# Building neighbour lists for a four-layer graph attention network: five kept row buffers, another place for one step and for the checks

## The chip, the cores and the metric

The kernel runs on one core of a Trainium2 chip. A core has five instruction engines, each with its own order of work: TensorE (PE in the profile, its weight loads PEld), VectorE (DVE), ScalarE (ACT), GpSimd (POOL) and SyncE (SP, which here only issues transfers). Data lies in SBUF and PSUM on the core and in HBM off it; transfers (DMA) are issued by an engine and run beside it. The metric is device time in microseconds (us), one number per execution.

## The reference

Four graph attention layers, each as "x = x + GAT(relu(layernorm(x)))", over one graph of 3327 nodes with 512 features. The adjacency matrix is int32, symmetric, with self loops; an edge is there with a chance of about 0.0048, so a node has some 17 neighbours, itself among them. The layers differ in their heads (8, 4, 1, 8), in the form of the weights, and in an ELU after the middle two.

```python
adj = (bernoulli(0.0024, (3327, 3327)) | its transpose | eye).astype(int32)

def gat(h, adj, W, a_src, a_dst):                 # one layer, one head shown
    Wh = h @ W
    e = leaky_relu((Wh @ a_src)[:, None] + (Wh @ a_dst)[None, :], 0.2)
    e = where(adj > 0, e, -inf)
    return softmax(e, over the neighbours) @ Wh   # then elu in layers 1 and 2

for i in range(4):
    h = maximum((x - mean) / sqrt(var + 1e-5), 0)
    x = x + gat(h, adj, *weights[i])
```

## The kernel before

The nodes are padded to 3328 and handled as 26 tiles of 128 rows, one row to an SBUF partition. Rather than work with the dense matrix, the kernel first turns it into lists of neighbours (`tile_gat_stack`, from L521), then runs the four layers by gathering the rows of neighbours from tables in HBM (`tile_gat_lists`). If the lists could not be right for the matrix at hand (a node with over 40 neighbours, too many nodes with many neighbours, or an entry that isn't 0 or 1), a dense version, `tile_gat_dense`, runs instead. A flag `bad`, computed with the lists, chooses between them.

**The list loop, L677 to L719.** For each tile t:

- SyncE loads the 128 adjacency rows `a` (1664 KB, three buffers, L682), and GpSimd multiplies them by `keys`, which fall from left to right: `key` (L683, three buffers) is 0 where there is no edge and names the column where there is one. VectorE adds BOOST on the diagonal, so that a node itself comes first (L687). ScalarE sums the rows of `a` into `total`, the number of neighbours (L689).
- VectorE cuts each row into 16 segments and takes the eight largest keys of each (L692, into `cand`). Between these 16 instructions stand the *pieces* of the tile before, made by `rest` (L653): nine in turn take the 40 largest out of its `cand` (`max` at L659, `match_replace` at L661), then `counted` (L632) lets ScalarE write the list `L[:, t, :]` and VectorE count the entries found into `held`, and `sorted_in` (L637) marks the bin of that count in `o`, has TensorE form, in `pn`, how many rows with that count stand ahead of each row, and in `count`, how many rows each bin holds so far (L639 to L643); ScalarE copies `count` to `sofar` for the next tile (L646). `placed` (L651) reads `pn` for VectorE; it stands at segment 8, for the tile before the one whose pieces run.
- In the same loop the features of layer 0 are made. The row of `x` is loaded into the middle of a wide row buffer `vx` by a DMA that ScalarE issues (L709 to L711). `centred_by_scalar` (L478 to L493) finds mean and variance on ScalarE: `nm` (L485), `xn` (L487), `squares` (L490), `ve` (L492). `features` (L666 to L673) then works on the tile before: TensorE transposes `xn` (L451), ScalarE copies the result with a relu (`hT`, L458), TensorE projects (`pv`, L469), GpSimd makes `rstd` out of `ve` (L432), ScalarE writes the projected row into the same `vx` (L669, L671), and SyncE stores it into the table `tabx` in HBM (L673). `vx` comes out of a rotating pool with four buffers.

A block `tc.manual_schedule` keeps the orders of GpSimd and VectorE as written in the loop. ScalarE, TensorE and SyncE are put in order by a scheduler when the program is built. So GpSimd has key of tile t+1, rstd of tile t, key of tile t+2, and so on, in a fixed order.

**After the loop, L717.** With nothing left to be interleaved with, the last steps run on their own: `last` (which is `placed` of tile 24), the eleven pieces of tile 25, then `placed` of tile 25.

**The ranks, L720 to L783.** Here the order of all engines but SyncE is as written. VectorE adds BOOST to the first column of `L` (L722), sums the bins (scan, L723) and gives each node its rank, which is stored into `tabx` (L724 to L729); `hi` and `lo` split the rank into tile and row. Then come the checks: `held` against `total` (L741, L742), the first neighbour against the node's own number (L744, L745), the bins against their limits (L747, L748), each summed into a column of `wrong`, and from these `bad` (L753). The rest, to L783, turns lists and ranks into index tables, with which the gathers of the layers run (L830).

Of the kernel before, what the change touches and what calls it, by code (L numbers as in the profile page):

```python
# [10 lines left out]
F32 = mybir.dt.float32  # L11
# [4 lines left out]
OP = mybir.AluOpType  # L16
AX = mybir.AxisListType
# [507 lines left out]
def tile_gat_stack(ctx: ExitStack, tc: tile.TileContext, x, adj, adjT, ws, avs, out):  # L525
# [35 lines left out]
    with ExitStack() as c1:  # L561
# [92 lines left out]
        def rest(t, cand):  # L654
# [8 lines left out]
            pieces.append(lambda: made.append(sorted_in(t)))  # L663
            return pieces, lambda: placed(t, made[0])

        def features(t, vx, xn, ve):  # L666
            pv = projected(nc, W, cut(nc, turned(nc, xn, ident, ps_t), work), ps_v)
            rstd = rooted(nc, ve, small, half)
            nc.scalar.activation(vx[:, :ROW].rearrange("p (s n) -> p s n", s=2), pv[:, :, :ROW // 2], AF.Copy,  # L669
                                 scale=rstd)  # L670
            nc.scalar.activation(vx[:, ROW + F:].rearrange("p (s n) -> p s n", s=2), pv[:, :, ROW // 2 - 8:ROW // 2],  # L671
                                 AF.Copy, scale=rstd)
            nc.sync.dma_start(tabx[t * P:(t + 1) * P, :], vx)  # L673

        count, pieces, last, normed, loads = None, [], None, None, []
        with tc.manual_schedule(engines={mybir.EngineType.Pool, mybir.EngineType.DVE}):
            for t in range(NT):  # L677
                a = apool.tile([P, NP], I32, name="a")
                key = kpool.tile([P, NP], I32, name="key")
                quarter = NP // 4 if t == 0 else NP  # L680
                for c in range(0, NP, quarter):
                    nc.sync.dma_start(a[:, c:c + quarter], adj[t * P:(t + 1) * P, c:c + quarter])  # L682
                    nc.gpsimd.tensor_tensor(key[:, c:c + quarter], a[:, c:c + quarter], keys[:, c:c + quarter], OP.mult)  # L683
                if t == 1:
                    W = Weights(nc, wpool, work, 0, ws, avs)
                dg = key[:, t * P:(t + 1) * P]
                nc.vector.tensor_add(dg, dg, boost)  # L687
                waste = once.tile([P, NP], mybir.dt.bfloat16, name="waste")
                nc.scalar.activation(waste, a, AF.Relu, accum_out=total[:, t:t + 1])  # L689
                cand = small.tile([P, SEGS * 8], F32, name="cand")  # L690
                for g in range(SEGS):
                    nc.vector.max(cand[:, g * 8:(g + 1) * 8], key[:, g * SEG:(g + 1) * SEG])  # L692
                    if g == SEGS // 2 and last is not None:
                        last()
                        last = None
                    elif g > 0 and pieces:
                        pieces.pop(0)()
                if t == 0:
                    constants()
                if t == 1:  # L700
                    while W.left:
                        W.fold()
                if t == 2:
                    own = late_constants()
                if t > 0:
                    last = then
                pieces, then = rest(t, cand)

                vx = work.tile([P, 2 * ROW], F32, name="vx", bufs=4)  # L709
                xt = vx[:, ROW:ROW + F]  # L710
                nc.scalar.dma_start(xt, x[t * P:(t + 1) * P, :])  # L711
                if normed is not None:
                    features(*normed)
                normed = (t, vx, *centred_by_scalar(nc, xt, small, work))
            features(*normed)
            for piece in [last, *pieces, then]:
                piece()  # L717

        with tc.manual_schedule(engines={mybir.EngineType.Pool, mybir.EngineType.PE,  # L719
                                         mybir.EngineType.DVE, mybir.EngineType.Activation}):  # L720

            nc.vector.tensor_scalar(L[:, :, 0], L[:, :, 0], BOOST, None, OP.add)  # L722
            nc.vector.tensor_tensor_scan(base[:, 1:], ones[:, :BINS], count, 0.0, OP.mult, OP.add)  # L723
            nc.vector.tensor_mul(o, o, base[:, :BINS].unsqueeze(1).to_broadcast([P, NT, BINS]))  # L724
            rank = small.tile([P, NT], F32, name="rank", bufs=1)
            nc.vector.tensor_reduce(rank, o, AX.X, OP.add)
            nc.vector.tensor_add(rank, rank, part)

            nc.sync.dma_start(tabx[:NP, :].rearrange("(t p) c -> p t c", p=P)[:, :, F // 2:F // 2 + 1],  # L729
                              rank.unsqueeze(2))  # L730
            hi = small.tile([P, NT], F32, name="hi", bufs=1)
            nc.vector.tensor_scalar(hi, rank, 1.0 / P, -(P - 1) / 2.0 / P, OP.mult, OP.add)
            nc.vector.tensor_scalar(hi, hi, ROUND, -ROUND, OP.add, OP.add)
            lo = small.tile([P, NT], F32, name="lo", bufs=1)
            nc.vector.scalar_tensor_tensor(lo, hi, -float(P), rank, OP.mult, OP.add)

            wrong = small.tile([P, 3], F32, name="wrong", bufs=1)
            m1 = small.tile([P, NT], F32, name="m1", bufs=2)  # L740
            nc.vector.tensor_tensor(m1, held, total, OP.not_equal)  # L741
            nc.vector.tensor_reduce(wrong[:, 0:1], m1, AX.X, OP.add)  # L742
            m1 = small.tile([P, NT], F32, name="m1", bufs=2)
            nc.vector.tensor_tensor(m1, own, L[:, :, 0], OP.not_equal)  # L744
            nc.vector.tensor_reduce(wrong[:, 1:2], m1, AX.X, OP.add)  # L745
            junk = small.tile([P, BINS], F32, name="junk")
            nc.vector.tensor_tensor(junk, base[:, :BINS], limit, OP.is_gt)  # L747
            nc.vector.tensor_reduce(wrong[:, 2:3], junk, AX.X, OP.add)  # L748
            pn = ps_n.tile([P, BANK], F32, name="pn", bufs=1)
            nc.tensor.matmul(pn[0:1, :3], ones[:, 0:1], wrong, start=True, stop=True)  # L750
            worst = small.tile([1, 1], F32, name="worst", bufs=1)
            nc.vector.tensor_reduce(worst, pn[0:1, :3], AX.X, OP.max)
            nc.vector.tensor_copy(bad, worst)  # L753


            for i, part_ in enumerate(slots.parts):
                t0, t1 = min(b[0] for b in part_.blocks), max(b[1] for b in part_.blocks)
                high = fixed[:, 304:512] if i == 0 else ps_k.tile([P, BANK], F32, name="high")
                high = high[:, :NT * (t1 - t0)].rearrange("p (t h) -> p t h", h=t1 - t0)
                nc.vector.tensor_tensor(high, ahead[:, t0:t1].unsqueeze(1).to_broadcast([P, NT, t1 - t0]),  # L760
                                        hi.unsqueeze(2).to_broadcast([P, NT, t1 - t0]), OP.is_equal)
                n = part_.columns
                if i == 0:
                    (_, _, k, _), = part_.blocks
                    every = once.tile([P, NT, n], F32, name="every")
                    nc.vector.tensor_tensor(every.rearrange("p t (h k) -> p t h k", k=k),
                                            L[:, :, :k].unsqueeze(2).to_broadcast([P, NT, t1 - t0, k]),
                                            high.unsqueeze(3).to_broadcast([P, NT, t1 - t0, k]), OP.mult)
                pi = ps_i.tile([P, BANK], F32, name="pi")
                for t in range(NT):  # L770
                    if i == 0:
                        rhs = every[:, t, :]
                        nc.vector.tensor_scalar(low[:, t, :], ahead, lo[:, t:t + 1], None, OP.is_equal)
                    else:
                        rhs = spare[:, t % 2, :]
                        for b0, b1, k, c in part_.blocks:
                            nc.vector.tensor_tensor(
                                rhs[:, c:c + (b1 - b0) * k].rearrange("p (t k) -> p t k", k=k),
                                L[:, t, :k].unsqueeze(1).to_broadcast([P, b1 - b0, k]),
                                high[:, t, b0 - t0:b1 - t0].unsqueeze(2).to_broadcast([P, b1 - b0, k]), OP.mult)  # L780
                    nc.tensor.matmul(pi[:, :n], low[:, t, :], rhs, start=(t == 0), stop=(t == NT - 1))
                nc.scalar.activation(part_.idx, pi[:, :n], AF.Copy)
                nc.scalar.activation(part_.twice, pi[:, :n], AF.Copy, scale=2.0)  # L783
# [655 lines left out]
```

## Time and profile before

| | us |
|---|---|
| median of three runs | 2492.9 (2492.3 to 2494.5) |
| the profiled execution | 2493.66 |
| its span, first to last instruction | 2491.9 |
| list loop and ranks, up to the first gather on GpSimd | 282.25 |
| VectorE's first work of the layers | 307.30 |
| start of the 26th, last key of GpSimd | 243.73 |
| store of the ranks | 266.19 |

The mean granted clock of TensorE was 0.945 of full speed. A profile comes from one execution, whose span is a little shorter than its device time. Lines of groups read: line of the kernel, engine, operation, output<-inputs, shape, count; then busy time, mean ns of one; then the idle time of the engine just before these instructions and what ended it. In a timeline a line has the start in us, the duration, engine, line and operation, and in brackets the idle time before it with its releaser. "ACTq" is the issue of a transfer by ScalarE. The table of windows gives the busy time of each engine in a stretch, with the number of instructions behind "x". An idle engine costs nothing unless the end hangs on it.

Over the whole span TensorE was busy for 2083.4 us (84%), VectorE for 1935.6 (78%), GpSimd for 1710.7 (69%), ScalarE for 911.6 (37%). From 310 us on, where the layers run, TensorE was busy for 1881.4 of 2181 us.

### The profile page before, as it was taken

The numbers are of one execution on the slowest core, as the hardware profiler recorded it, in microseconds if no ns is written. First come the engines' busy times: TensorE is split into PE (matmuls) and PEld (weight loads), VectorE is DVE, ScalarE is ACT, GpSimd is POOL, SyncE is SP. The second block draws the span as 40 slices with busy tenths as digits, with TensorE's granted clock in tenths as the row PEclk, the third lists the DMA queues.
The fourth block names the chain that finished last, engine by engine and source line by source line (L and its number), as shares of the span: only waits on it lengthen the run. The fifth ranks groups of instructions, "written<-read, shape, count | busy, mean of one in ns | idle before, by whom it ended". The sixth has DMA issues, their size and how long they took to land. (4 is left out here: it accounts for less than half of the span.)

```text
span 2491.9 us, 26810 instructions
## 1 busy us (share of the span) xinstructions
PE 2083.4 (84%) x6832; PEld 1163.5 (47%) x6832; DVE 1935.6 (78%) x5004; ACT 911.6 (37%) x2506; POOL 1710.7 (69%) x1700
## 2 busy tenths in 40 slices
PE   3776789999898855999999986869696699999897
PEld 1655445555444422555555543434353454455453
DVE  7887787887767735788888876978979488787776
ACT  4777123343321102433333323433333343333330
POOL 7798367777777756776777746655546377777775
PEclk9888899999999987999999998979898899999999
DMA  6797579999887777877888858867777488888885
GB/s 231 280 298 240 173 219 291 284 298 296 277 270 237 231 194 239 261 244 228 247 258 258 252 162 264 271 194 239 211 229 212 134 253 247 246 250 250 240 243 173
DMA packets 262490, 599.55 MB, mean 241 GB/s; under 512 B 103923, under 2 KB 121331, under 8 KB 257974
## 3 DMA queue, kind: packets, MB, share of 16 engines
q0 software_dynamic: 126128, 438.08, 57.7%
q1 hardware_dynamic: 132454, 152.86, 19.2%
q10 hardware_dynamic: 3744, 6.82, 0.8%
q8 instruction: 55, 0.90, 0.1%
q14 instruction: 109, 0.89, 0.1%
HBM read 547.96 MB, written 49.65 MB: 240 GB/s over the span
## 5 line engine op out<-in xcount | busy, mean ns | idle before, releaser
L917 PE MATMUL bank<-m,ident 128*128 128x512 f32 x2608 | 1204.6, 608 | 132.6 <-DVE m L912 132.0
L912 DVE TENSOR_TENSOR m<-g,pw 128x512 f32<-128x512 f32 x1304 | 810.6, 681 | 137.3 <-ACT pw L886 131.5
L830 POOL DMA_INDIRECT g<-tab,idxb x734 | 698.2, 951 | 284.7 <-issue 173.1
L917 PEld LDWEIGHTS bank<-m,ident 128*128 128x128 f32 x2608 | 483.3, 193 | 714.0 <-issue 347.5
L469 PE MATMUL pv<-w,hT 128*128 128x264 f32 x1664 | 438.5, 420 | 67.4 <-ACT hT L458 38.8
L886 ACT ACTIVATE pw<-z 128x32 f32<-128x32 f32 (+5 forms) x434 | 84.0, 194 | 987.2 <-DVE z L885 987.1
L469 PEld LDWEIGHTS pv<-w,hT 128*128 128x128 f32 x1664 | 340.3, 208 | 170.3 <-ACT hT L458 44.1
L830 POOL DMA_INDIRECT g<-tabx,twiceb x342 | 324.2, 948 | 105.1 <-issue 78.6
L830 POOL DMA_INDIRECT g<-tab,idxa x297 | 283.6, 955 | 145.1 <-issue 78.2
L1133 PE MATMUL whole<-ve,em 128*128 128x512 f32 x468 | 222.4, 623 | 41.4 <-DVE em L1119 38.5
L883 DVE TENSOR_TENSOR z<-g,pw 128x32 f32<-128x32 f32 (+5 forms) x434 | 74.9, 173 | 189.3 <-DMA g<-tab,idxa 83.0
L683 POOL TENSOR_TENSOR key<-a,keys 128x3328 int32<-128x3328 int32 (+1 forms) x29 | 189.1, 6525 | 14.5 <-DVE cand L692 11.8
L907 DVE SCALAR_TENSOR_TENSOR bank<-g,pw,bank 128x512 f32<-128x512 f32 x243 | 183.2, 754 | 6.8
L1133 PEld LDWEIGHTS whole<-ve,em 128*128 128x128 f32 x468 | 90.1, 199 | 152.3 <-issue 90.7
L692 DVE MAX8 cand<-key 128x8 f32<-128x208 int32 x416 | 143.7, 363 | 0.1
L830 POOL DMA_INDIRECT g<-tabx,twicea x99 | 94.4, 954 | 67.8 <-issue 32.7
L451 PE MATMUL pt<-ident,xn 128*128 128x128 f32 x416 | 68.6, 291 | 85.5 <-ACT hT L458 31.0
L451 PEld LDWEIGHTS pt<-ident,xn 128*128 128x128 f32 x416 | 53.6, 149 | 122.6 <-issue 48.4
L1108 ACT ACTIVATE r<-low,mc,b 128x384 f32<-128x384 f32 x78 | 52.6, 674 | 153.5 <-DVE em L1119 116.6
L432 POOL TENSOR_TENSOR rstd<-ve,half 128x1 f32<-128x1 f32 x52 | 31.8, 611 | 107.3 <-DVE ve L970 61.7
L1242 ACT ACTIVATE r<-low,spare 128x256 f32<-128x256 f32 x208 | 98.9, 476 | 5.1
L885 DVE SCALAR_TENSOR_TENSOR z<-z 128x32 f32<-128x32 f32 (+5 forms) x434 | 78.8, 182 | 15.3 <-DVE z L883 0.4
(175 smaller groups left out, 2111.5 us busy)
## 6 DMA issues: line engine op xcount, KB each, us to landing
a<-in_adj SPq DMA_DIRECT2D x25, 1664.0 KB, 9.0
tab<-v SPq DMA_DIRECT2D x78, 264.0 KB, 4.0
ve<-tab SPq DMA_DIRECT2D x78, 264.0 KB, 4.5
g<-tab SPq DMA_DIRECT2D x66, 264.0 KB, 4.7
tabx<-vx SPq DMA_DIRECT2D x26, 528.0 KB, 9.5
g<-tab,idxb POOLq DMA_INDIRECT x734, 3.9
low<-tab SPq DMA_DIRECT2D x52, 132.0 KB, 3.4
room<-tab SPq DMA_DIRECT2D x52, 132.0 KB, 3.6
```

Of the source, the lines that this page charges most:

```text
L451: nc.tensor.transpose(pt[:, k, :], xn[:, k * P:(k + 1) * P], ident)
L469: nc.tensor.matmul(pv[:, s, :HF + 8], hT[:, k, :], W.w[:, k, s, :], start=(k == 0), stop=(k == KC - 1))
L683: nc.gpsimd.tensor_tensor(key[:, c:c + quarter], a[:, c:c + quarter], keys[:, c:c + quarter], OP.mult)
L692: nc.vector.max(cand[:, g * 8:(g + 1) * 8], key[:, g * SEG:(g + 1) * SEG])
L830: nc.gpsimd.indirect_dma_start(out=out_, out_offset=None, in_=table, in_offset=bass.IndirectOffsetOnAxis(ap=which, axis=0))
L885: nc.vector.scalar_tensor_tensor(z, z, SLOPE, z, OP.mult, OP.max)
L886: nc.scalar.activation(self.wt[:, k0:k0 + n, :H], z, AF.Exp)
L907: nc.vector.scalar_tensor_tensor(acc, v, w, acc, OP.mult, OP.add)
L912: nc.vector.tensor_tensor(m[:, q, :].rearrange("p (s h d) -> p s h d", s=2, d=D), v.rearrange("p s (h d) -> p s h d", d=D), wt[:, k0 + q, ...
L917: nc.tensor.matmul(self.po, ident, m[:, q, :], start=(k0 + q == 0), stop=(k0 + q == K - 1))
L1133: nc.tensor.matmul(tl.po.rearrange("p (s m) -> p s m", s=2), e[:, q * P:(q + 1) * P], v.rearrange("p (s m) -> p s m", s=2)[:, :, :F // 2], ...
L1242: nc.scalar.activation(self.r[:, h, :], self.a[:, g, :], AF.Relu, bias=-1.0, scale=self.b[:, j, g:g + 1])
```

## The change

Line numbers here are those of the kernel before.

1. The row buffers are no longer taken from the rotating pool of four. Five tiles `vx0` to `vx4` are kept for the whole stage, and tile t uses number t modulo 5. A list `loads` that nothing used goes.
2. After the loop, `last` no longer runs first, but as the fifth of the steps, behind the first four pieces of tile 25.
3. The boost of the first column (L722) and the first two checks (L740 to L745) become a function `check`, which runs after the pieces of tile 25 and ahead of its `placed`. So they leave the second block, in which all engines' orders are as written, for the first, in which only those of GpSimd and VectorE are. The third check and `bad` stay where they were.

```diff
+        wrong = small.tile([P, 3], F32, name="wrong", bufs=1)
+
+        def check():
+            nc.vector.tensor_scalar(L[:, :, 0], L[:, :, 0], BOOST, None, OP.add)
+            m1 = small.tile([P, NT], F32, name="m1", bufs=2)
+            nc.vector.tensor_tensor(m1, held, total, OP.not_equal)
+            nc.vector.tensor_reduce(wrong[:, 0:1], m1, AX.X, OP.add)
+            m1 = small.tile([P, NT], F32, name="m1", bufs=2)
+            nc.vector.tensor_tensor(m1, own, L[:, :, 0], OP.not_equal)
+            nc.vector.tensor_reduce(wrong[:, 1:2], m1, AX.X, OP.add)
+
...
-        count, pieces, last, normed, loads = None, [], None, None, []
+        rows = [once.tile([P, 2 * ROW], F32, name=f"vx{i}") for i in range(5)]
+        count, pieces, last, normed = None, [], None, None
...
-                vx = work.tile([P, 2 * ROW], F32, name="vx", bufs=4)
+                vx = rows[t % 5]
                 xt = vx[:, ROW:ROW + F]
                 nc.scalar.dma_start(xt, x[t * P:(t + 1) * P, :])
...
             features(*normed)
-            for piece in [last, *pieces, then]:
+            pieces[4:4] = [last]
+            for piece in [*pieces, check, then]:
                 piece()
...
-            nc.vector.tensor_scalar(L[:, :, 0], L[:, :, 0], BOOST, None, OP.add)
             nc.vector.tensor_tensor_scan(base[:, 1:], ones[:, :BINS], count, 0.0, OP.mult, OP.add)
...
-            wrong = small.tile([P, 3], F32, name="wrong", bufs=1)
-            m1 = small.tile([P, NT], F32, name="m1", bufs=2)
-            nc.vector.tensor_tensor(m1, held, total, OP.not_equal)
-            nc.vector.tensor_reduce(wrong[:, 0:1], m1, AX.X, OP.add)
-            m1 = small.tile([P, NT], F32, name="m1", bufs=2)
-            nc.vector.tensor_tensor(m1, own, L[:, :, 0], OP.not_equal)
-            nc.vector.tensor_reduce(wrong[:, 1:2], m1, AX.X, OP.add)
```

## The prediction, made before the changed kernel ran

> **What bounds the kernel now.** I first cut the run into stretches with the table of busy time by window. The list building fills the first 310 us, the four layers the rest, and the change touches only the list building. In its long middle no engine is full:
>
> ```profile
> core 0: us, PE busy (x) PEld busy (x) DVE busy (x) ACT busy (x) POOL busy (x), PEclk, DMA share, GB/s
> 90.00:243.00 153.00, 111.81 (x501) 90.97 (x500) 124.98 (x615) 120.69 (x250) 136.36 (x35) 0.87 0.83 277
> ```
>
> GpSimd (POOL) is nearest to full, 136.4 of 153 us. The groups of this window (busy, mean ns, idle before) say what it does and what it lacks:
>
> ```profile
> L683 POOL TENSOR_TENSOR key<-a,keys 128x3328 int32<-128x3328 int32 x18 | 130.6, 7254 | 0.0
> L432 POOL TENSOR_TENSOR rstd<-ve,half 128x1 f32<-128x1 f32 x17 | 9.3, 548 | 16.0 <-ACT ve L492 7.0 <-DVE cand L692 5.6 <-DVE top L659 3.2
> ```
>
> All idle time stands before `rstd`, whose only moving input is ScalarE's `ve`; the view names VectorE for part of it, but `rstd` reads nothing of VectorE's, so I book all of it to `ve`. POOL's order is fixed: key of tile t+1, rstd of tile t, key of tile t+2. POOL's timeline shows the two great holes and the small steady ones:
>
> ```profile
> 62.05 7.26 POOL L683 TENSOR_TENSOR key<-a,keys 128x3328 int32<-128x3328 int32 x1 [11.77 <-DVE cand L692]
> 78.27 0.55 POOL L432 TENSOR_TENSOR rstd<-ve,half 128x1 f32<-128x1 f32 x1 [8.95 <-DVE top L659]
> 78.78 7.25 POOL L683 TENSOR_TENSOR key<-a,keys 128x3328 int32<-128x3328 int32 x1
> ...
> 225.60 0.55 POOL L432 TENSOR_TENSOR rstd<-ve,half 128x1 f32<-128x1 f32 x1 [0.82 <-ACT ve L492]
> 226.11 7.25 POOL L683 TENSOR_TENSOR key<-a,keys 128x3328 int32<-128x3328 int32 x1
> ```
>
> ScalarE's timeline says why `ve` is late in both places:
>
> ```profile
> 66.31 0.34 ACTq L711 DMA_DIRECT2D vx<-in_x  x1
> 73.92 0.62 ACT L485 ACTIVATE waste<-vx 128x512 f32<-128x512 f32 x1
> 78.00 0.19 ACT L492 ACTIVATE ve<-squares 128x1 f32<-128x1 f32 x1
> ...
> 223.25 0.21 ACT L646 ACTIVATE sofar<-count 128x41 f32<-128x41 f32 x1 [1.74 <-PE count L643]
> 224.21 0.64 ACT L490 ACTIVATE waste<-xn 128x512 f32<-128x512 f32 x1
> 225.30 0.22 ACT L492 ACTIVATE ve<-squares 128x1 f32<-128x1 f32 x1
> ```
>
> At 66.31 the row of tile 4 is first loaded: it has to reuse the buffer of tile 0, so its `ve` is there at 78.2 and POOL has stood since 69.3. At 223.25 `squares` and `ve` of the next tile stand behind `sofar`, which waits for counts that need VectorE's work on the newest key: POOL's key ends, 7.6 us of VectorE and TensorE, 2.1 us of ScalarE, then `rstd`. That is longer than one 7.77 us turn of POOL. Last, VectorE's end of the stage, from which every later step of the lists hangs:
>
> ```profile
> 261.96 0.19 DVE L722 TENSOR_SCALAR L<-L 128x26 f32<-128x26 f32 x1
> 262.66 0.20 DVE L651 SCALAR_TENSOR_TENSOR junk<-pn,o 128x41 f32<-128x41 f32 x1 [0.50 <-PE pn L640]
> 263.10 0.24 DVE L723 TENSOR_TENSOR_SCAN base<-ones,count 128x41 f32<-128x41 f32 x1 [0.24 <-PE count L643]
> ...
> 266.72 0.18 DVE L741 TENSOR_TENSOR m<-held,total 128x26 f32<-128x26 f32 x1
> 267.36 0.19 DVE L747 TENSOR_TENSOR junk<-base,limit 128x41 f32<-128x41 f32 x1
> ```
>
> **What the Trainium skill says.** "DMA: Bandwidth & Descriptors", section "Anatomy of one DMA": a wait for a semaphore is kept on the issuing sequencer, not in the DMA engine, and one transfer costs about 2.0 us plus bytes over 436 GB/s. So a row load stands in ScalarE's own order; and 262,144 bytes make 2.6 us as an estimate, where the view of the row buffers gives 2.7 as the least. Its section "Issuing engines are not separate DMA queues" says that transfers of all issuers share the same 16 engines; the trace agrees, for beside the adjacency the same load takes 8.9:
>
> ```profile
> DMA to landing us min/median/max: 2.7/8.9/11.5
> ```
>
> "SBUF — State Buffer", section "SBUF: two separate sides": a VectorE operation with two SBUF inputs and a GpSimd operation lock each other out. It shows here (the product at 42.52 took 7.36 us against 0.69, until POOL's key was done), but the moved checks run after POOL's last `rstd` at 252.94.
>
> **Part by part.** In the built program POOL's order is the same; VectorE's differs only at the end of the stage; ScalarE's and TensorE's, which a scheduler makes, change all through. After the lists all engines keep their order, and the waits that differ there, from another memory layout, are for work long done. So what the stage saves, the run saves.
>
> *Five rows, start.* 26 loads and 26 stores as before. The fifth load goes out at the start; 256 KB beside 1664 KB that take some 4 us is at most 0.6 us for a neighbour, and POOL waits 11.8 us at 50 anyway: 0. Key 6 (78.78 before) then needs: POOL free at 69.31 plus 0.52 for rstd 4; key buffer free at 69.0 (VectorE's tile 3); adjacency of tile 6, issued 57.61, at 9.0 (its median) 66.6. So 69.8, 8.9 earlier. Key 7 needs rstd 5, and tile 5 now takes the place of tile 4 (load 66.31, `ve` 78.2), and the adjacency issued at 70.85, there at 79.5 to 79.9: start 79.5, against 87.14. Key 8 needs `ve` 6: its load now is the one of 75.42, landed 79.96; behind it in ScalarE's new order nm 0.75, total 2.96, row writes 0.75, hT 0.5, xn 0.7, squares 0.75, kept and ve 0.3, makes 86.7, and POOL is free at 86.75. Key 8 at 87.3 against 96.04: 8.7 saved.
>
> *Five rows, steady.* Before, key 8 to key 25 took 243.73 - 96.04 = 147.7, 8.69 each. In the new order `ve` t is queued behind `sofar` t-2, in places with the row write of t-1 between, instead of behind `sofar` t-1: a whole turn earlier. POOL alone needs 7.25 + 0.52 = 7.77, 17 turns 132.1. What is left of waits: ScalarE's work for a tile sums to 7.0 us (total 2.96; nm, xn, squares 2.2; row 0.75; hT 0.5; six small ones 0.6), so it has only 0.8 to spare, and between `ve` 9 and `ve` 10 its order now has two totals (11, 12). Carried from `ve` 9 at 108.6: totals 11 and 12 make 6, two row writes 1.5, hT, nm, xn, squares, hT 3.2, small ones 0.5, and 0.6 until pv 9 is ready: 120.4, where POOL is free at 117.7: 2.7. At 13, 14 and 19 to 23 `ve` slips behind the next row write, which I put at 4 together. For row loads that land later (ScalarE waited for those 14.0 us in all before) I add 3.5. Waits 10.2, key 25 at 87.3 + 132.1 + 10.2 = 229.6 against 243.73: 14.1 saved.
>
> *Last counts later.* `placed` 24 stood at 258.05, and its counts ended at 257.99: nothing to win; four pieces (1.4 us) later it has cover for TensorE's new order, where counts 24 come behind seven of eight products of tile 25. 0; without that cover some 1 us.
>
> *Checks.* Five VectorE instructions and no DMA: the boost and the four of 266.72 to 267.36, 0.64. They fill the waits of 0.50 and 0.24 before `placed` and the scan, which costs 0.1 to 0.3 there, and leave 0.64 behind the scan: 0.4 saved. But the boost reads ScalarE's list of tile 25, which is now queued behind the row write of tile 25, which needs its products. If these end as before (262.2), the boost starts at 263.4, not 261.96, and `placed` behind it at 264.4: a loss of 1.1. If the stage runs ahead, none. Between -0.4 and +1.1 I take 0.
>
> Sum: 14. The profiled execution took 2493.66 us (span 2491.9, 1.8 around it), 0.8 above the median of 2492.9; 2493.7 - 14 = 2479.7 for it, **2479** for the median. Its own range, waits from 5 to 15 us: 2474 to 2484.
>
> **Rivals.** *The rate stays at 8.69,* since ScalarE (7.0 of 7.77) or the DMAs (share 0.83 at 277 GB/s; at 7.77 it would be 0.93) pace it. For it: ScalarE's waits for row loads. Against: single turns of 7.73 and 7.92 in POOL's timeline (113.93, 121.66, 129.58). Only 8.7 is saved: 2484, 2483 to 2487. *No waits at all:* key 25 at 219.4, 24.3 saved, 2469; against it the two totals in a row. *Slower:* for tiles 17 to 21 the next row load is queued up to 2.6 us behind the nm of the row before, elsewhere right behind it (0.75), so one load is under way at a time. If a load takes 8.9 from its own issue, a turn is 11.5 for five tiles and 9.65 for twelve: 3.7 x 5 + 1.9 x 12 = 41 more on 132.1, less 4 that `ve` is ahead; key 25 at 256.6, 13 later, 2506. It decides from about 8.1 us. Against it: loads issued later than the adjacency of their turn landed sooner (issued 98.01, used 104.21; 75.42, 79.96), for they end with that burst. *It doesn't do what it says:* the scheduler's order gives the start back, within 5 us of 2493.
>
> **Numbers.** Likeliest 0.58, rate stays 0.18, no waits 0.12, given back 0.05, slower 0.07. 2470 to 2487 leaves out half of "no waits" and the last two. A change of 0.2%, 5 us, is what a measurement can tell: faster 0.88, same 0.05, slower 0.07.
>
> **What would show it.** Key 6 near 70 and key 8 near 87; rstd's idle time from key 8 on near 10 us, not 17, the largest near tile 10; the five checks ahead of the scan; 2226 us from the rank store to the end as now. I am wrong if row loads keep ScalarE waiting over 3 us a tile, or if key 6 stays at 78.

## The result: 8.0 us faster, and where they came from

| | before | changed |
|---|---|---|
| median of six runs, us | 2492.87 (2489.87 to 2494.50) | 2484.85 (2482.29 to 2489.33) |
| ratio, 95% interval | | 0.9970 (0.9958 to 0.9983) |
| profiled execution, span | 2491.9 | 2483.4 |
| key 6 of GpSimd starts | 78.78 | 70.77 |
| key 8 | 96.04 | 88.61 |
| key 25, the last | 243.73 | 236.01 |
| sum of the ranks (VectorE) | 265.98 | 258.65 |
| first gather | 282.25 | 273.46 |
| first gather to the end of the span | 2209.7 | 2209.9 |

The time was inside the forecast range of 2470 to 2487, but near the rival "the rate stays", not the likeliest case: 14 us were forecast, 8 came, and the likeliest case's own range ended at 2484. The last row of the table says where to look: behind the first gather the two kernels take the same time. All of the difference is in the list building.

The hole ahead of key 6 is gone, as the prediction had it; the one of 11.77 us ahead of key 5 is not. GpSimd's timeline of the changed kernel (start, duration, then in brackets the idle time before):

```profile
63.04 7.26 POOL L695 TENSOR_TENSOR key<-a,keys 128x3328 int32<-128x3328 int32 x1 [11.77 <-DVE cand L704]
70.26 0.54 POOL L432 TENSOR_TENSOR rstd<-ve,half 128x1 f32<-128x1 f32 x1
70.77 7.26 POOL L695 TENSOR_TENSOR key<-a,keys 128x3328 int32<-128x3328 int32 x1
...
113.95 7.27 POOL L695 TENSOR_TENSOR key<-a,keys 128x3328 int32<-128x3328 int32 x1
125.86 0.55 POOL L432 TENSOR_TENSOR rstd<-ve,half 128x1 f32<-128x1 f32 x1 [4.64 <-ACT ve L492]
126.38 7.26 POOL L695 TENSOR_TENSOR key<-a,keys 128x3328 int32<-128x3328 int32 x1
```

Before, `rstd` of tile 4 stood 8.95 us idle ahead of 78.27; here it starts as soon as the key at 63.04 is done. But further down there is a hole of 4.64 us that was not there before. To compare the steady part, take the same stretch of work of both, key 8 to key 25, in the table of busy time by window, first of the kernel before (core busy times of PE, PEld, DVE, ACT, POOL with the instructions behind "x", clock, DMA share, GB/s):

```profile
96.00:244.00 148.00, 107.86 (x487) 88.00 (x488) 121.20 (x596) 116.27 (x244) 132.29 (x36) 0.87 0.84 279
```

and of the changed one:

```profile
88.00:236.00 148.00, 115.41 (x515) 95.19 (x514) 125.29 (x617) 120.05 (x251) 132.39 (x35) 0.85 0.84 292
```

The fifth busy number is GpSimd's: 132.29 and 132.39 of the same 148 us. The groups of GpSimd in this window of the changed kernel agree:

```profile
L432 POOL TENSOR_TENSOR rstd<-ve,half 128x1 f32<-128x1 f32 x18 | 10.0, 558 | 15.6 <-ACT ve L492 11.7 <-DVE cand L704 3.4 <-DVE cand L661 0.2
```

15.6 us idle before `rstd` (16.9 before the change, over the same number of tiles). So the fifth buffer took the hole ahead of key 6 away and left the steady waits as large as they were. They are in other places, though. Before, 13 of the 17 turns had a wait of 0.5 to 2.4 us; now ten have 0.2 us or less, two have 0.8, and five hold nearly all: 1.7, 4.7, 1.4, 3.4 and 2.5 us. ScalarE's timeline at the largest (start, duration, operation) shows what stands before `ve`:

```profile
113.15 0.20 ACT L492 ACTIVATE ve<-squares 128x1 f32<-128x1 f32 x1
113.26 2.96 ACT L701 ACTIVATE waste<-a 128x3328 bf16<-128x3328 int32 x1
...
117.39 0.70 ACT L680 ACTIVATE vx<-pv,rstd 128x528 f32<-128x528 f32 x1 [0.85 <-PE pv L469]
...
119.47 0.72 ACT L487 ACTIVATE xn<-vx,nm 128x512 f32<-128x512 f32 x1
120.10 2.96 ACT L701 ACTIVATE waste<-a 128x3328 bf16<-128x3328 int32 x1
...
123.61 0.70 ACT L680 ACTIVATE vx<-pv,rstd 128x528 f32<-128x528 f32 x1 [0.24 <-PE pv L469]
...
124.49 0.63 ACT L490 ACTIVATE waste<-xn 128x512 f32<-128x512 f32 x1
...
125.58 0.21 ACT L492 ACTIVATE ve<-squares 128x1 f32<-128x1 f32 x1
```

Between `ve` 9 (113.15) and `ve` 10 (125.58) there are two sums of adjacency rows (L701) and two row writes (L680). The second sum stands between `xn` of tile 10 and its `squares`, though all that `squares` needs is there at 120.1. GpSimd had finished its key at 121.2 and stood until 125.86.

The end of the stage in the changed kernel, VectorE's timeline:

```profile
253.99 0.26 DVE L637 TENSOR_SCALAR o<-fixed,held 128x41 f32<-128x41 f32 x1
254.28 0.19 DVE L669 TENSOR_SCALAR L<-L 128x26 f32<-128x26 f32 x1
...
255.59 0.24 DVE L735 TENSOR_TENSOR_SCAN base<-ones,count 128x41 f32<-128x41 f32 x1 [0.70 <-PE count L643]
255.75 0.15 DVE L675 TENSOR_REDUCE wrong<-m 128x1 f32<-128x26 f32 x1
255.82 0.19 DVE L651 SCALAR_TENSOR_TENSOR junk<-pn,o 128x41 f32<-128x41 f32 x1
```

The boost (L669) comes right behind the pieces, with no wait for ScalarE's list; the checks fill part of the wait for the counts. From the start of key 25 to the sum of the ranks it is 22.64 us (22.25 before), to the product that opens the index tables (`every`) 24.75 (24.99 before): 0.4 longer to the one place and 0.2 shorter to the other, in one execution of each.

### The profile page after: what moved, and what is told of

The parts are those of the page before. It is cut to its first block, busy times and chain, and to the rows that moved or that the text cites. A ratio compares the mean times of both kernels' runs of the same rounds, so it can differ in the third digit from the quotient of the medians.

```text
span 2483.4 us, 26799 instructions
## 1 busy us (share of the span) xinstructions
PE 2077.1 (84%) x6832; PEld 1161.7 (47%) x6832; DVE 1935.1 (78%) x5004; ACT 910.9 (37%) x2506; POOL 1709.5 (69%) x1700
## 5 line engine op out<-in xcount | busy, mean ns | idle before, releaser
L922 PE MATMUL bank<-m,ident 128*128 128x512 f32 x2608 | 1202.3, 607 | 131.9 <-DVE m L917 131.2
```

The source lines that it names most:

```text
L922: nc.tensor.matmul(self.po, ident, m[:, q, :], start=(k0 + q == 0), stop=(k0 + q == K - 1))
```

## The experiments

A theory from these lines, "order": with five buffers GpSimd's waits are set by where ScalarE's order puts `ve`, not by how fast rows, DMA or TensorE can go. Its rival, "pace": a tile takes 8.7 us on average whatever the order, since something else holds it. A second question was which part of the change is worth what.

In the tables a wait is the distance between the starts of two keys less 7.77 us (7.25 for the key, 0.52 for `rstd`), summed over the 17 turns from key 8 to key 25. "Drain" is the time from the start of key 25 to the sum of the ranks. These come from one profiled execution of each kernel. Two kernels were run twice (e6 and e13, e9 and e12): their pairs differ by up to 0.6 us in key 25, 1.7 in the waits and 1.3 in the drain, so smaller differences tell nothing. The ratios are to the kernel before in the same session, where it took 2493.5 us beside e1, e2, e5 and e6 and 2493.4 beside e10 to e13.

| kernel | median, us | ratio to before (95%) | key 6 | key 8 | key 25 | waits | drain |
|---|---|---|---|---|---|---|---|
| before | 2492.9 | | 78.8 | 96.0 | 243.7 | 15.6 | 22.3 |
| changed | 2484.9 | 0.9970 (0.9958 to 0.9983) | 70.8 | 88.6 | 236.0 | 15.3 | 22.6 |
| e1 five rows only | 2484.9 | 0.9968 (0.9956 to 0.9981) | 70.4 | 89.3 | 236.1 | 14.7 | 22.9 |
| e2 moved steps only | 2492.8 | 0.9998 (0.9990 to 1.0006) | 79.4 | 97.2 | 243.7 | 14.4 | 23.8 |
| e5 six rows | 2495.5 | 1.0009 (1.0003 to 1.0016) | 71.1 | 86.5 | 246.2 | 27.6 | 22.5 |
| e6 five rows, ve ahead | 2477.7 | 0.9938 (0.9926 to 0.9951) | 70.8 | 87.5 | 221.3 | 1.8 | 29.0 |
| e13 the same again | 2474.8 | 0.9930 (0.9917 to 0.9943) | 70.8 | 89.0 | 221.2 | 0.1 | 27.8 |
| e12 six rows, ve ahead | 2474.6 | 0.9924 (0.9911 to 0.9937) | 71.7 | 87.2 | 219.1 | -0.2 | 27.9 |
| e11 e6 with the end reordered | 2477.2 | 0.9937 (0.9924 to 0.9950) | 70.7 | 89.4 | 222.7 | 1.3 | 27.5 |
| e10 e12 with the end reordered | 2475.6 | 0.9924 (0.9911 to 0.9937) | 71.0 | 86.5 | 222.9 | 4.3 | 27.9 |

Four runs (e3, e7, e8, e9) were made in another session, in which every kernel, the one before included, took some 3010 to 3046 us. The record names another chip for it; whether the chip as such or its condition made the difference, the runs do not tell.

| kernel | median, us | ratio to before (95%) | key 6 | key 8 | key 25 | waits | drain |
|---|---|---|---|---|---|---|---|
| before, there | 3046.4 | | | | | | |
| e3 pool of five | 3033.1 | 0.9962 (0.9941 to 0.9984) | 70.6 | 87.7 | 238.4 | 18.7 | 22.8 |
| e7 e6 with counts first | 3031.8 | 0.9956 (0.9935 to 0.9976) | 70.6 | 87.4 | 221.5 | 2.1 | 29.0 |
| e8 four rows, ve ahead | 3035.8 | 0.9974 (0.9953 to 0.9995) | 79.1 | 97.1 | 236.1 | 6.9 | 25.4 |
| e9 six rows, ve ahead | 3010.0 | 0.9889 (0.9849 to 0.9928) | 71.4 | 86.9 | 219.7 | 0.7 | 29.1 |

The list building takes there what it took in the first session (key 25 of e9 and e12, the same kernel: 219.7 and 219.1), so its positions can be compared over both tables; the layers do not, and so these four times cannot.

### e1 and e2: which part is it?

e1 gives the kernel before the five rows and nothing else. e2 is the changed kernel with the pool of four put back:

```diff
-                vx = work.tile([P, 2 * ROW], F32, name="vx", bufs=4)
+                vx = rows[t % 5]          # e1, on the kernel before, with the line that makes the five rows
...
-                vx = rows[t % 5]
+                vx = work.tile([P, 2 * ROW], F32, name="vx", bufs=4)    # e2, on the changed kernel
```

> The kernel before with the five row buffers alone; the last steps and the checks stay where they were. In the built program its ScalarE and TensorE orders are those of the changed kernel. If the fifth buffer is the whole of the gain: 2485 us, 8 under before, GpSimd's 26th key near 236 (before 243.7), key 6 near 71. If half of the gain came from the moved steps: about 2489.

> The changed kernel with the row buffers back in the rotating pool of four; only the moved step and the moved checks are left. If they are worth nothing that can be measured: 2493, within 1.5 us of before, and the VectorE work from the 26th key to the ranks as long as before within 0.5 us. If they carry half of the gain: 2489. In the trace: rank sum 0.3 to 0.4 us later behind the key, the first large product of the index tables 0.2 to 0.3 us earlier.

e1 took 2484.93 us, the whole gain; e2 2492.75, no measurable one. Both as the first branch said, but for one detail: the drain of e2 was 1.5 us longer than before to the sum of the ranks and 0.9 longer to `every` (25.9 against 25.0), where a gain of 0.2 to 0.3 was expected for the latter. Its VectorE stood 1.39 us before the last `placed` for `pn`. That is hardly more than the 1.3 us by which the drain of one kernel differs between two executions, and the time does not show it. Between e1 and the changed kernel the moved steps are worth 0.8 us to `every` (25.6 against 24.75), again inside that scatter. So the moved steps are worth nothing that can be measured; the fifth buffer is the change.

### e6: put ve ahead

One rule more for the order in which ScalarE gets its instructions, no instruction added: from tile 9 on, the sum of tile t is issued behind `ve` of tile t-1.

```diff
-                nc.scalar.activation(waste, a, AF.Relu, accum_out=total[:, t:t + 1])
+                with tc.issue_after(marks[t - 1].ins) if t > 8 else ExitStack():
+                    nc.scalar.activation(waste, a, AF.Relu, accum_out=total[:, t:t + 1])
...
-                normed = (t, vx, *centred_by_scalar(nc, xt, small, work))
+                xn, ve, done = centred_by_scalar(nc, xt, small, work)    # done: the instruction of ve
+                marks.append(done)
+                normed = (t, vx, xn, ve)
```

> The changed kernel with one more rule for the order of ScalarE: from tile 9 on the sum of adjacency rows of tile t is issued behind ve of tile t-1, so that no ve has two of these sums, or a sum and a row write, between it and the ve before. No instruction is added. Theory 'order' (the 15 us that GpSimd still waits between keys 8 and 25 come from places where ScalarE's order puts ve late): turns of 7.8 us throughout, 26th key at 223 to 227 instead of 236.0, time 2473 to 2477. Theory 'pace' (DMA at 0.84 or the chain of TensorE and ScalarE can't go faster than 8.7 us a tile): the waits come back in other places, 26th key at 234 or later, time within 3 us of 2485.

Key 25 came at 221.33, a little before the interval that "order" gave, and the waits fell from 15.3 to 1.8 us. GpSimd's groups from key 8 to key 25:

```profile
L696 POOL TENSOR_TENSOR key<-a,keys 128x3328 int32<-128x3328 int32 x18 | 130.6, 7258 | 0.5 <-DMA a<-in_adj 0.5
L432 POOL TENSOR_TENSOR rstd<-ve,half 128x1 f32<-128x1 f32 x18 | 9.8, 546 | 1.9 <-ACT ve L492 1.0 <-DVE top L659 0.5 <-DVE cand L706 0.2
```

And the window from 90 us to the last key (busy times of PE, PEld, DVE, ACT, POOL; then clock, DMA share, GB/s):

```profile
90.00:221.00 131.00, 100.56 (x478) 83.53 (x477) 121.02 (x598) 110.39 (x234) 128.78 (x34) 0.89 0.90 318
```

"Pace" falls: with the same work, GpSimd runs at 7.87 us a turn, full at 128.8 of 131 us, and the DMAs bring 318 GB/s where 292 seemed to be what they gave. The 15 us were a matter of the built order. Not of ScalarE's order alone, though: the rule names ScalarE, but the scheduler made another order for TensorE with it. In the changed kernel the counts stand in the middle of the products of most tiles. In e6 the products of tiles in the middle of the stage stand unbroken ahead of the counts (all 16 records of a tile in a row, at 113.50, 120.40, 128.74 and 135.63 us), and from key 8 to key 25 ScalarE waited 1.6 us for products, not 7.7 as in the changed kernel. What each of the two orders is worth was not separated.

The time was 2477.73 us, 7.1 under the changed kernel and just over the 2473 to 2477 expected, and 2474.84 in a second run (e13). But key 25 came 14.7 earlier. Nearly half of that went in the drain, which grew from 22.6 to 29.0 us. VectorE's timeline of e6 there:

```profile
235.90 0.20 DVE L651 SCALAR_TENSOR_TENSOR junk<-pn,o 128x41 f32<-128x41 f32 x1 [2.03 <-PE pn L640]
...
243.73 0.20 DVE L651 SCALAR_TENSOR_TENSOR junk<-pn,o 128x41 f32<-128x41 f32 x1 [3.43 <-PE pn L640]
```

VectorE waits for `pn` of tiles 23 and 24, which TensorE has behind feature products. When the last key is done (228.6), three rows of features are still to be written in e6, at 231.1, 239.0 and 245.2; in the changed kernel (243.3) it is two, at 245.2 and 251.5. Their products share TensorE with the last counts.

The same kernel once more, beside the later runs:

> Five rows with ve ahead once more, beside the others on one chip: 15 to 17 us under before as in its first run, key 25 at 221 to 223.

It came 18.5 us under the kernel before, more than expected, with key 25 at 221.2.

### e5, e9 and e12: six rows

```diff
-        rows = [once.tile([P, 2 * ROW], F32, name=f"vx{i}") for i in range(5)]
+        rows = [once.tile([P, 2 * ROW], F32, name=f"vx{i}") for i in range(6)]
...
-                vx = rows[t % 5]
+                vx = rows[t % 6]
```

> The changed kernel with six kept row buffers in turn. Theory 'order': what counts is the order that ScalarE gets with it; in the built program ve is behind a sum and a row write for tiles 12, 14, 16, 18, 20, so GpSimd waits some 5 us at each, the 26th key comes near 244 and the time is near 2493, the gain lost. Theory 'buffers' (rows still come too late with five): 2485 or less.

2495.5 us, with key 25 at 246.2: a sixth buffer loses all that the fifth gained. The waits are where the order said, 4.95, 5.17, 4.02, 4.66 and 3.76 us in five turns. ScalarE's timeline at one of them:

```profile
148.32 0.72 ACT L487 ACTIVATE xn<-vx,nm 128x512 f32<-128x512 f32 x1
154.77 2.98 ACT L701 ACTIVATE waste<-a 128x3328 bf16<-128x3328 int32 x1 [5.73 <-DMA a<-in_adj]
...
158.74 0.62 ACT L490 ACTIVATE waste<-xn 128x512 f32<-128x512 f32 x1
...
159.91 0.21 ACT L492 ACTIVATE ve<-squares 128x1 f32<-128x1 f32 x1
```

`xn` is done at 149; the sum behind it waits 5.73 us for adjacency rows, and `squares` and `ve`, which need nothing of it, wait with it. With the same six rows and the rule of e6:

> The rule of ve ahead with six row buffers kept. Theory 'order': the 27.6 us of waits that six buffers alone had were all the scheduler's order of ScalarE, so with the rule they fall under 4 us, the 26th key comes at 219 to 222 instead of 246.2, and the time is 2475 to 2479, as with five. Theory 'buffers' (a sixth load under way harms by itself, through the DMAs): waits stay over 12, time over 2484.

Key 25 came at 219.7 and the waits fell from 27.6 to 0.7: the sixth buffer does no harm by itself. The time, 36 us under before, was more than the list building can give and came from the slower session, so it was run again:

> The six rows with ve ahead once more, since its first time came from a chip on which every kernel took some 3040 us and scattered by 40. The list building there ended 19 us earlier than in the kernel before on the first chip (first gather 263.0 against 282.3). If only the list building is behind its gain: 14 to 19 us under before. If the 36 us of the first time were real: over 25 under before, on a part that the change doesn't touch.

2474.55 us, 18.8 under before, the first branch. The 36 us were not the kernel's own; what gave e9 the rest on the other chip stays open. e12 is the fastest of the kernels run, level with e13 inside the intervals.

### e8 and e3: four rows with the rule, and a pool of five

```diff
+        rows = [once.tile([P, 2 * ROW], F32, name=f"vx{i}") for i in range(4)]    # e8, with e6's rule
+                vx = rows[t % 4]
...
-                vx = work.tile([P, 2 * ROW], F32, name="vx", bufs=4)
+                vx = work.tile([P, 2 * ROW], F32, name="vx", bufs=5)              # e3, on the kernel before
```

> The rule of ve ahead with only four row buffers kept. The hole ahead of key 6 stays (key 6 near 79, key 8 near 96). If the rule works by itself, by ScalarE's order alone: waits from key 8 on fall from 15 us to some 3 to 5, 26th key at 232 to 236, and with some 6 us given back in the drain as with five buffers, time 2485 to 2489. If the rule needs the fifth buffer (rows come too late with four): waits stay over 10, time 2491 to 2494.

> The kernel before with its rotating pool raised from four buffers to five, nothing else. In the built program its orders are those of the five kept rows but for five places on ScalarE. If only the number of buffers counts: 2485 as with kept rows, 26th key near 236. If it matters that the rows are kept and taken in turn: a difference of over 2 us from 2485.

e8: key 6 stays at 79.1, and the waits fall to 6.9 us, of which 5.6 stand in one turn; more than the 3 to 5 expected, but far under the 10 of the other branch. So hole and waits are two things: with four buffers the hole stays whatever the order, and the order sets most of the waits. e3: key 6 at 70.6 and key 25 at 238.4, two us behind the kept rows and with 18.7 us of waits in nearly the same places. Times in that session can't tell 2 us. That the rows are kept, rather than dealt out by a pool, is not what helps.

### e7, e10 and e11: the drain

Three attempts to get back what the drain took. e7 has TensorE do the products of tile 24 behind the counts of tile 23 (in the code `counts[-2]` at the first place below, and `counts[-1]` round the second `features` where it stood), those of tile 25 behind the counts of tile 24. e10 and e11 (on six and on five rows) go one tile further:

```diff
-                    features(*normed)
+                    with tc.issue_after(counts[-1].ins) if t == NT - 1 else ExitStack():   # e10, e11
+                        features(*normed)
...
-            features(*normed)
             pieces[4:4] = [last]
-            for piece in [*pieces, check, then]:
+            for piece in pieces:
                 piece()
+            with tc.issue_after(counts[-1].ins):
+                features(*normed)
+            check()
+            then()
```

> The kernel with ve ahead, and one more rule: TensorE gets the products of tile 24 behind the counts of tile 23, those of tile 25 behind the counts of tile 24. With ve ahead alone the stretch from the 26th key to the sum of the ranks took 29.0 us (changed kernel 22.6, before 22.3), and VectorE stood 2.0 and 3.4 us before placed 23 and 24 for counts that were queued behind feature products. If this queue is what gave half of the gain back: the stretch shrinks to 24 to 26 us, the two waits go, time 2473 to 2476. If something else holds the end of the stage (ScalarE's last rows, the stores): the stretch stays over 28 and the time within 1.5 of 2478.

> Six rows with ve ahead, and the end of the loop reordered: TensorE gets the products of tile 24 behind the counts of tile 24 and those of tile 25 behind the counts of tile 25, so that no count is queued behind products whose own inputs are late. If that queue on TensorE is what lengthened the drain: from the 26th key to the sum of the ranks 24 to 26 us instead of 29, waits before placed 23 to 25 under 1 us each but the last, time 3 to 5 us under six rows with ve ahead. If the stores of the last rows become the end: the ranks come earlier, the first gather does not, and the time is within 1 us.

> The same end of the loop with five rows and ve ahead. From the 26th key to the sum of the ranks 24 to 26 us (29.0 with ve ahead alone); time 3 to 5 us under five rows with ve ahead, so about 18 to 20 under before. If not the queue on TensorE: 29 us again and the same time.

All three missed: drains of 29.0, 27.9 and 27.5 us, where e6 and e13 had 29.0 and 27.8 and e12 27.9. The times did not gain either: e10 took 2475.6 us beside 2474.6 for e12, e11 2477.2 beside 2474.8 for e13, and e7 has no like kernel in its session. One of e11's six executions took 5494.4 us; it is not in the median, there is no trace of it, and its cause stays open. The queue on TensorE was not the whole of it. TensorE's timeline of e11:

```profile
237.47 0.52 PE L639 MATMUL pn<-o,upper 128*128 128x41 f32 x2 [2.19 <-DVE o L637]
...
241.01 5.52 PE L469 MATMUL pv<-w,hT 128*128 128x264 f32 x16 [0.69 <-ACT hT L458]
246.37 0.31 PE L639 MATMUL pn<-o,upper 128*128 128x41 f32 x2
```

`pn` of tile 24 (237.47) now waits for VectorE, as it should. But the products of tile 24 come next, 5.5 us of them, and `pn` of tile 25, ready to go at 242, comes behind at 246.4; VectorE stood 4.03 us for it. The wait went from one tile to the next. What would clear the drain, products split around the last counts or less feature work left by then, was not tried.

## Why the prediction was right, and where it was off

**The bound was read rightly.** GpSimd's chain of keys and `rstd` set the stage, and `rstd` hung on ScalarE's `ve`. e6 shows it: with `ve` in time, GpSimd is full.

**Five rows, start: right, with one wrong zero.** Forecast were key 6 at 69.8 and key 8 at 87.3; they came at 70.77 and 88.61. About 1 us of this is the step "the fifth load goes out at the start ... POOL waits 11.8 us at 50 anyway: 0". Key 1 began at 15.25 instead of 14.38, and keys 2 to 5 were each 0.96 to 0.99 late. GpSimd's timeline has both, first of the kernel before:

```profile
14.38 7.24 POOL L683 TENSOR_TENSOR key<-a,keys 128x3328 int32<-128x3328 int32 x1 [0.44 <-DMA a<-in_adj]
```

and of the changed one:

```profile
15.25 7.23 POOL L695 TENSOR_TENSOR key<-a,keys 128x3328 int32<-128x3328 int32 x1 [1.04 <-DMA a<-in_adj]
```

The 11.77 us at key 5 are no cover. They end when VectorE has folded the weights and searched tile 2, and VectorE's own start hangs on the same early keys; so the wait moved as a whole (62.05 to 63.04) and was 11.77 us in both kernels. That the fifth load is what made the early adjacency late is likely, since every kernel with five or six rows has key 1 at 15.1 to 15.4 and those with four (before, e2, e8) at 14.4 to 14.8; the 256 KB alone make 0.65 us, as an estimate from the 406 GB/s that the DMAs moved, at a full share, from 5 to 30 us in the kernel before. SyncE's first weight loads went off at other times too (7.46 us instead of 5.66 for the first), and the two were not separated.

**Five rows, steady: the step that failed.** "Waits 10.2" was 15.3. Term by term: tile 10, the largest as forecast, was put at 2.7 and measured 4.7. The row writes ahead of `ve` (tiles 13, 14, 19 to 23), put at 4 together, measured 7.5. The 3.5 for "row loads that land later" has 3.1 to match it (tiles 7, 15 and small ones), but it was not the loads. In the stretches shown above, 96 to 244 us before and 88 to 236 us after, ScalarE's wait for row loads fell from 12.4 to 9.4 us and its wait for counts from 15.0 to 9.1, while its wait for TensorE's products, ahead of the row writes, rose from 1.9 to 7.7. Tile 21 shows it best. First TensorE's timeline, then ScalarE's:

```profile
209.88 0.71 PE L469 MATMUL pv<-w,hT 128*128 128x264 f32 x2 [2.43 <-ACT hT L458]
...
211.74 6.22 PE L469 MATMUL pv<-w,hT 128*128 128x264 f32 x14
```

```profile
212.69 2.97 ACT L701 ACTIVATE waste<-a 128x3328 bf16<-128x3328 int32 x1
...
218.05 0.70 ACT L680 ACTIVATE vx<-pv,rstd 128x528 f32<-128x528 f32 x1 [2.31 <-PE pv L469]
...
219.56 0.20 ACT L492 ACTIVATE ve<-squares 128x1 f32<-128x1 f32 x1
```

and GpSimd's:

```profile
219.84 0.55 POOL L432 TENSOR_TENSOR rstd<-ve,half 128x1 f32<-128x1 f32 x1 [2.50 <-ACT ve L492]
```

The counts stand between the two parts of the products, the row write waits 2.31 us for the second part, and GpSimd waits 2.5 us for the `ve` behind it. Ahead of the `ve` of tiles 7, 10, 19 and 21 such waits come to 1.05, 1.09, 1.31 and 2.31 us, 5.8 together. The forecast had 0.6 for them, at tile 10, and nothing elsewhere; the waits as a whole were 5.1 over it. That is a sum over one trace, not a test.

Two more things play a part. One is TensorE's granted clock: the products ahead of tiles 7, 19 and 21 ran at 0.56, 0.52 and 0.53 of full speed, so that 14 records took 6.22 us, where they took 3.38 at a clock of 1.00 (from 118.79 us). How much of these waits is the clock's, and how much the order's, no run separates; in e6 one tile's products ran at 0.70 (from 120.40 us) and GpSimd did not wait. The other: at tile 19 two sums of adjacency rows stood between one `ve` and the next, as at tile 10, and the forecast counted only a row write there.

So the step that failed is the price of what stands ahead of `ve`: an instruction put ahead of `ve` costs not only its own length but what it waits for itself.

**The rival that hit the number had the wrong reason.** "The rate stays at 8.69" gave 2484, and the rate was 147.4 / 17 = 8.67. But it put this down to ScalarE's load or the DMAs as a pace. e6 and e12 ran 17 turns in 133.9 and 131.9 us on the same work. It hit the number by luck: the order cost 15 us again, in other places. That a rate stays equal is no sign that something holds it: 15 us in thirteen small waits became 15 us in five larger ones and two small.

**Last counts, checks: right.** Forecast 0 each; e2 has a ratio of 0.9998 (0.9990 to 1.0006). The feared loss, the boost waiting for ScalarE's last list, did not occur: the stage ran ahead, with the last row write at 251.46 instead of 262.2.

**"Slower" did not come.** Row loads issued behind others did not stretch the turns for tiles 17 to 21; three of the turns there had no wait at all.

**After the lists: right.** 2226 us from the store of the ranks to the end were forecast; the store went out at 258.86, which leaves 2224.5.

## What to carry to other kernels

Where an engine's order is made by a scheduler, a buffer more is not a buffer more: it is a new order for that engine. Here five buffers gained 8 us, six lost 2, and with one rule on the order five gained 16 to 19 and six 19. So compare the built orders, look for a short instruction that others wait for (`ve`, 0.2 us) behind long or waiting ones that nobody waits for (the sum, 3 us), and pin that before counting buffers. And before calling a wait a cover, ask what ends it: if that moves with the work to be covered, it hides nothing.

## What was not expected of the hardware

The slower session. The kernel before took 3046 us there and 2493 otherwise. The list building was as fast as ever; the layers were not. Windows of one kernel (six rows, ve ahead), first e12:

```profile
0.00:300.00 300.00, 194.38 (x843) 144.89 (x844) 254.03 (x1046) 181.29 (x383) 234.75 (x141) 0.92 0.73 258
300.00:2470.00 2170.00, 1874.06 (x5991) 1011.22 (x5989) 1680.04 (x3960) 728.94 (x2123) 1479.19 (x1559) 0.95 0.79 241
```

then e9, from the slower session:

```profile
0.00:300.00 300.00, 193.72 (x834) 143.82 (x834) 245.06 (x1023) 179.02 (x374) 231.84 (x138) 0.91 0.72 255
300.00:3000.00 2700.00, 2035.95 (x5998) 1072.85 (x5998) 1685.92 (x3981) 733.53 (x2133) 1481.79 (x1562) 0.87 0.65 194
```

In the layers TensorE's granted clock was 0.87 instead of 0.95 and its busy time 9% longer, the DMAs moved 194 GB/s instead of 241, and VectorE, ScalarE and GpSimd were busy for the same time within 1%. TensorE's 160 us more don't make up the 530 us by which the layers were longer; the rest is waits, and why they grew stays open.
